# x in a ring of five tiles, loads in pairs, four stores a tile and products in place: a bilinear interaction kernel on one core

## The chip, the cores and the metric

The kernel runs on one core of one Trainium2 chip. The metric is device time in microseconds (us), the median over several executions; lower is better. Each run comes with a state: in the slow one, the cores show a lower clock and the time is some per cent longer.

## The reference

For 4096 samples of 32 features with 64 numbers each, every pair i < j of features (496 pairs) has its own 64 x 64 matrix W. The output is (x_i W_p) * x_j for every pair p, in float32.

```python
idx_i, idx_j = np.triu_indices(F, k=1)          # F = 32: 496 pairs
vi = inputs[:, idx_i, :]
vj = inputs[:, idx_j, :]
vidots = jnp.einsum('bpd,pde->bpe', vi, W)      # W: (496, 64, 64)
return vidots * vj                              # 4096 x 496 x 64 float32, 520 MB
```

42 MB are read and 520 MB are written, so this is a kernel of stores.

## The kernel before

A tile is 128 samples; two tiles are a block. TensorE turns a tile of x, multiplies it with W into PSUM, and VectorE multiplies each PSUM result by x_j into an output buffer. For seven values of i, ScalarE copies the PSUM result to a temporary and GpSimd multiplies it by x_j instead. When a group of pairs is complete, SyncE stores the buffer. There are three output buffers of 105 pairs and five stores a tile.

```python
bounds = [0, p0[3], p0[6] + CH, p0[11], p0[17], NP]     # five groups a tile
xpool = ctx.enter_context(tc.tile_pool(name="xpool", bufs=2))    # two blocks of x
opool = ctx.enter_context(tc.tile_pool(name="opool", bufs=3))
...
        if i in aside and c0 == 0:                      # i = 1, 3, 5, 7, 9, 11, 13
            tmp = dst
            if t >= LEAD:
                tmp = tpool.tile([P, CH, 2, E2], F32, tag="tmp", name=f"tmp_{s}")
            nc.scalar.copy(tmp, src)
            nc.gpsimd.tensor_mul(dst, tmp, xj)
        else:
            nc.vector.tensor_mul(dst, src, xj)
```

Half of the later blocks are loaded by one DMA on ScalarE's queue. The other half are loaded by GpSimd in four DMAs: 120 rows, a tiny read into a scratch tile, and the last 8 rows in two halves. Their names in the code (`load_fifteen`, `turn_engines`) say that this is meant to spare one of the 16 DMA engines; the traces have no engine numbers.

```python
def load_fifteen(blk: int):
    rows = rows_of(x, blk).rearrange("(p k) f d -> p k f d", k=NB)
    dst = xs[blk]

    def part(ps: slice, fs: slice):
        tc.keep_in_program_order(nc.gpsimd.dma_start(out=dst[ps, :, fs, :], in_=rows[ps, :, fs, :]))

    part(slice(0, SWR), slice(0, F))                    # 120 rows
    turn_engines(1)                                     # the scratch read
    for h in range(2):                                  # 8 rows, in two halves of the features
        part(slice(SWR, P), slice(h * F // 2, (h + 1) * F // 2))
```

Two words that come up often: a DMA has "landed" when all its bytes are in place and it raises its semaphore, a counter on which an engine can wait; a queue is "drained" when nothing is left in it.

## Time and profile before

| | before |
|---|---|
| median time | 1333.64 us (4 runs, 1333.56 to 1333.72) |
| busy share: PE, DVE, ACT, POOL | 86%, 72%, 35%, 42% |
| DMA engines | busy from start to end, mean 424 GB/s |
| stores | 161, of 928 to 3360 KB |
| loads of x after the lead | 14 events: 7 on ScalarE's queue, 7 by GpSimd |

PE is TensorE, DVE is VectorE, ACT is ScalarE, POOL is GpSimd. A busy share averages over the span, and here the row that stays full in every slice is that of the DMA engines: the kernel ends when the bytes are out. Any change then has two ways to act: on the rate at which bytes move, and on moments in which nothing is queued for them.

### The profile page before, as it was taken

What the parts mean: (1) busy time and instruction counts of PE and PEld (TensorE: products, weight loads), DVE (VectorE), ACT (ScalarE), POOL (GpSimd) and SP (SyncE); (2) the same over time, 40 slices, a digit from 0 to 9 for tenths busy, and PEclk for the clock granted to TensorE, in tenths of its full rate; (3) what the DMA queues carried; (4) which work ended last, traced back from release to release, by engine and by line L of the source; (5) the groups of instructions that cost most, each with busy time, mean ns of one, the idle gap of its engine ahead of it and who ended that gap; (6) DMA issues with size and microseconds to landing.
All of it is one profiled execution on the core that took longest, in us unless ns stands there. A gap on an engine that the chain in (4) does not pass through costs nothing.

```text
span 1329.5 us, 16690 instructions
## 1 busy us (share of the span) xinstructions
PE 1139.7 (86%) x6656; PEld 605.9 (46%) x6656; DVE 950.9 (72%) x1258; ACT 471.7 (35%) x627; POOL 558.4 (42%) x264
## 2 busy tenths in 40 slices
PE   6989879878898888888989888888897988879994
PEld 4555435444444444444444444444444444444442
DVE  5878768757777677776768777676775777767774
ACT  4463323333333333333333333333333333333331
POOL 1752424444433444333453334533335443444432
PEclk9999999989999899998999999999998999989997
DMA  9999999999999999999999999999999999999998
GB/s 390 432 404 425 428 423 431 426 429 430 420 428 425 431 430 417 430 422 429 431 419 428 424 433 429 416 430 423 431 431 417 430 418 429 431 415 432 429 427 371
DMA packets 28142, 563.13 MB, mean 424 GB/s; under 512 B 3760, under 2 KB 3760, under 8 KB 4112
## 3 DMA queue, kind: packets, MB, share of 16 engines
q1 hardware_dynamic: 24192, 532.69, 94.2%
q0 software_dynamic: 2864, 14.70, 2.7%
q10 hardware_dynamic: 1008, 14.68, 2.6%
q8 instruction: 52, 0.85, 0.2%
q14 instruction: 26, 0.21, 0.0%
HBM read 41.94 MB, written 520.09 MB: 423 GB/s over the span
## 4 chain that ended last, share of the span: by engine, by line
DMA 55%; PE 19%; DVE 15%; POOL 4%; issue 4%; ACT 1%; DVEq 0%; POOLq 0%; SPq 0%; ACTq 0%
DMA out_dram<-ot 55%; PE ps L259 17%; DVE ot L279 15%; POOL ot L277 4%; PE ptx L159 1%; POOL rp L139 1%; ACT tmp L276 0%; DMA xs<-in_r_inputs_dram 0%; PE ptw L148 0%; DVE rp L139 0%; DVEq L279 0%; ACT xT L163 0%; ACT xT L164 0%; ACT xT L165 0%; POOLq L277 0%
## 5 line engine op out<-in xcount | busy, mean ns | idle before, releaser
L279 DVE TENSOR_TENSOR ot<-ps,xs 128x1024 f32<-128x1024 f32 (+15 forms) x1248 | 936.0, 806 | 348.7 <-DMA out_dram<-ot 193.4
L259 PE MATMUL ps<-wT,xT 64*128 64x512 f32 (+12 forms) x6016 | 1049.0, 489 | 157.4 <-DVE ot L279 152.5
L259 PEld LDWEIGHTS ps<-wT,xT 64*128 64x128 f32 x6016 | 535.9, 196 | 609.9 <-DVE ot L279 366.4
L277 POOL TENSOR_TENSOR ot<-tmp,xs 128x1024 f32<-128x1024 f32 x203 | 479.2, 2361 | 693.6 <-ACT tmp L276 520.0
L276 ACT COPY tmp<-ps 128x1024 f32<-128x1024 f32 x203 | 205.5, 1012 | 472.9 <-PE ps L259 436.6
L163 ACT COPY xT<-ptx 128x512 f32<-128x512 f32 x128 | 75.0, 586 | 318.3 <-PE ptx L159 318.3
L159 PE MATMUL ptx<-ident,xs 128*128 128x128 f32 x512 | 84.4, 288 | 9.9 <-DMA xs<-in_r_inputs_dram 6.5
L159 PEld LDWEIGHTS ptx<-ident,xs 128*128 128x128 f32 x512 | 54.0, 141 | 82.2 <-DVE ot L279 57.4
L165 ACT COPY xT<-ptx 64x512 f32<-64x512 f32 x128 | 74.6, 582 | 1.6
L164 ACT COPY xT<-ptx 64x512 f32<-64x512 f32 x128 | 73.9, 577 | 1.5
L277 POOL TENSOR_TENSOR ot<-ot,xs 128x1024 f32<-128x1024 f32 x21 | 49.9, 2378 | 52.2 <-ACT ot L276 52.1
L276 ACT COPY ot<-ps 128x1024 f32<-128x1024 f32 x21 | 21.3, 1013 | 24.4 <-PE ps L259 15.1
L148 PE MATMUL ptw<-ident,rp 128*128 128x128 f32 (+1 forms) x128 | 18.9, 303 | 5.8 <-DVE rp L139 5.8
L148 PEld LDWEIGHTS ptw<-ident,rp 128*128 128x128 f32 (+1 forms) x128 | 16.1, 159 | 14.6 <-DVE rp L139 5.2
L139 DVE COPY rp<-raw 128x1024 f32<-128x1024 f32 x9 | 14.7, 1650 | 10.6 <-DMA raw<-in_L_rec_W_dram 10.6
L151 ACT COPY wT<-ptw 128x1024 f32<-128x1024 f32 (+1 forms) x15 | 14.8, 984 | 13.8 <-PE ptw L148 10.9
L105 POOL DMA_DIRECT2D xs<-in_r_inputs_dram x21 | 13.3, 637 | 0.0
L97 POOL DMA_DIRECT2D scratch<-in_r_inputs_dram x9 | 8.2, 911 | 0.3 <-issue 0.3
L139 POOL COPY rp<-wT 112x1024 f32<-112x1024 f32 x4 | 7.9, 1978 | 0.0
L139 ACT COPY rp<-raw 128x1024 f32<-128x1024 f32 x3 | 6.0, 1987 | 1.9 <-DMA raw<-in_L_rec_W_dram 1.9
L151 DVE COPY wT<-ptw 128x1024 f32<-128x1024 f32 x1 | 1.2, 1225 | 3.0 <-PE ptw L148 3.0
L163 ACT ACT_TABLE_LOAD x1 | 1.3, 1283 | 0.7 <-PEq L303 0.7
(6 smaller groups left out, 0.9 us busy)
## 6 DMA issues: line engine op xcount, KB each, us to landing
out_dram<-ot SPq DMA_DIRECT2D x64, 3360.0 KB, 16.4
out_dram<-ot SPq DMA_DIRECT2D x32, 3168.0 KB, 15.6
out_dram<-ot SPq DMA_DIRECT2D x32, 3104.0 KB, 17.0
out_dram<-ot SPq DMA_DIRECT2D x31, 2880.0 KB, 17.0
xs<-in_r_inputs_dram ACTq DMA_DIRECT2D x7, 2048.0 KB, 18.7
xs<-in_r_inputs_dram POOLq DMA_DIRECT2D x7, 1920.0 KB, 25.0
raw<-in_L_rec_W_dram SPq DMA_DIRECT2D x3, 2048.0 KB, 13.8
xs<-in_r_inputs_dram SPq DMA_DIRECT2D x2, 1024.0 KB, 10.4
```

Source lines behind the costliest of these rows:

```text
L105: tc.keep_in_program_order(nc.gpsimd.dma_start(out=dst[ps, :, fs, :], in_=rows[ps, :, fs, :]))
L139: ins = copy(rp[:r], src[:, k * EU : (k + 1) * EU])
L148: nc.tensor.transpose(pt[:, n, :r], rp[:r, n].rearrange("p h d -> p (h d)"), ident[:r, :r])
L151: copy(home_of(c, r)[:, :, k * EU : (k + 1) * EU], pt[:, :, :r].rearrange("p e r -> p r e"))
L159: nc.tensor.transpose(pt[:, u, :], xs[blk][:, k, f : f + 2, :].rearrange("p f d -> p (f d)"), ident)
L163: copy(xT[:, 0], pt)
L164: copy(xT[D:, 1], pt[:D])
L165: copy(xT[:D, 1], pt[D:])
L259: nc.tensor.matmul(ps[:, h, lo - pa : hi - pa, :], xT[blk, kt, i // RUN][h * D : (h + 1) * D, (i + h) % 2, i % RUN // 2, :], wT[home][h * ...
L276: nc.scalar.copy(tmp, src)
L277: nc.gpsimd.tensor_mul(dst, tmp, xj)
L279: nc.vector.tensor_mul(dst, src, xj)
```

## The change

Its intent: x gets a ring of five tile slots in one long buffer in place of two block buffers, so that two blocks can be loaded together, on two queues, once every four tiles. What that and the in-place products free in memory goes to larger output buffers (127 pairs), and so to four stores a tile. The lead (the first three tiles, in which W is also turned and whose groups are made in turns) gets six groups instead of five. `load_fifteen` keeps its four DMAs but writes into the ring. Cut to its core:

```diff
-    bounds = [0, p0[3], p0[6] + CH, p0[11], p0[17], NP]
+    lead = [0, p0[3], p0[6], p0[9], p0[13], p0[18], NP]
+    later = [0, p0[4], p0[9], p0[15] + 10, NP]
...
-    xpool = ctx.enter_context(tc.tile_pool(name="xpool", bufs=2))
-    tpool = ctx.enter_context(tc.tile_pool(name="tpool", bufs=4))
-    opool = ctx.enter_context(tc.tile_pool(name="opool", bufs=3))
+    xb = const.tile([P, 5 * FD + 3 * GAP], F32, tag="xb", name="xb")
+    ob = const.tile([P, 3 * cap1, D], F32, tag="ob", name="ob")
...
-        dst = xs[blk]                       # in load_fifteen
+        dst = x_block(blk)
...
-    LATE = 6
-    loads = {place[blk * NB, LATE]: blk + 1 for blk in range(2, NBLK - 1)}
+    LATE = 1
+    loads = {place[2 * NB * e - 1, LATE]: 2 * e for e in range(1, NBLK // 2)}
...
         if s in loads:
-            new_x(loads[s])
-            if loads[s] in fifteen:
-                load_fifteen(loads[s])
-            else:
-                load_x(loads[s], nc.scalar)
+            load_x(loads[s], nc.scalar)
+            load_fifteen(loads[s] + 1)
...
-            tmp = dst
-            if t >= LEAD:
-                tmp = tpool.tile([P, CH, 2, E2], F32, tag="tmp", name=f"tmp_{s}")
-            nc.scalar.copy(tmp, src)
-            nc.gpsimd.tensor_mul(dst, tmp, xj)
+            nc.scalar.copy(dst, src)
+            nc.gpsimd.tensor_mul(dst, dst, xj)
```

## The prediction

> **What bounds the kernel now.** I read the slices of the page first, then its DMA queues, then the chain, then stretches of the span side by side.
>
> ```profile
> span 1329.5 us, 16690 instructions
> PE 1139.7 (86%) x6656; PEld 605.9 (46%) x6656; DVE 950.9 (72%) x1258; ACT 471.7 (35%) x627; POOL 558.4 (42%) x264
> ...
> DMA  9999999999999999999999999999999999999998
> ...
> q1 hardware_dynamic: 24192, 532.69, 94.2%
> q0 software_dynamic: 2864, 14.70, 2.7%
> q10 hardware_dynamic: 1008, 14.68, 2.6%
> ...
> DMA 55%; PE 19%; DVE 15%; POOL 4%; issue 4%; ACT 1%; DVEq 0%; POOLq 0%; SPq 0%; ACTq 0%
> ```
>
> The 16 DMA engines are busy from start to end (94.2 + 2.7 + 2.6% for stores, SP's loads and x), and no compute engine is above 86%. So the bytes set the end: 563.13 MB, which the change leaves as they are. What can move is the rate and the idle time of the DMA engines. Five stretches, as busy time of each engine, then granted clock, DMA share and GB/s:
>
> ```profile
> 199.50:262.30 62.80, 56.86 (x348) 30.42 (x350) 48.65 (x70) 22.35 (x31) 25.28 (x11) 0.97 1.00 431
> 262.30:281.20 18.90, 12.97 (x62) 6.24 (x58) 9.09 (x9) 5.79 (x7) 7.07 (x3) 0.91 1.00 419
> 350.80:382.80 32.00, 26.31 (x145) 14.57 (x144) 21.89 (x28) 10.46 (x15) 15.49 (x9) 0.89 1.01 418
> 90.00:95.00 5.00, 5.00 (x38) 2.73 (x36) 3.13 (x6) 3.77 (x5) 3.79 (x2) 1.00 0.62 264
> 1315.00:1329.50 14.50, 0.00 (x0) 0.00 (x0) 0.00 (x0) 0.00 (x0) 0.00 (x0) 0.50 0.68 293
> ```
>
> Stores alone run at 431 GB/s, near 430 over all stretches without loads. A load on ScalarE's queue costs (1 - 419/431) x 18.9 = 0.5 us, one on GpSimd's queue (1 - 418/431) x 32 = 1.0 us: 7 + 7 of them, some 10 us. 563.13 MB at 430 is 1310 us, so all losses together are 20 us: 10 in loads, about 5.5 in the first 125 us (nearly 3 of it the hole around 80 to 95 us), 4 in the uneven end. That is all that a change which moves no bytes can win.
>
> **What the change adds is a wait, and only the order of instructions shows it.** The second of two blocks is loaded by GpSimd in four DMAs: 120 rows, a 4-byte scratch read, then 8 rows in two halves. Before, the halves went out back to back. After, the last of the four waits for the third to land (semaphore names cut):
>
> ```
> before: 8x2x1024 load, 8x2x1024 load, multiply, multiply
> after:  8x2x1024 load (raises SW7 to 16), WAIT SW7 >= 16, 8x2x1024 load, multiply i=1, multiply i=3
>         SyncE: store of the tile's first group waits for GpSimd's count = that second multiply
> ```
>
> The halves do not overlap, but they interleave over the two rows of a partition, so their ranges do; the dependency tracking over one long buffer takes that for a write after a write. It is so in all seven loads. GpSimd's in-place multiplies stand behind it, and a tile's first group cannot be stored without two of them. How long such a wait is, the kernel before shows in the GpSimd timeline (start, duration) and in the DMA issues (KB each, us to landing):
>
> ```profile
> 349.22 0.79 POOL L105 DMA_DIRECT2D xs<-in_r_inputs_dram  x1
> 350.00 0.99 POOL L97 DMA_DIRECT2D scratch<-in_r_inputs_dram  x1
> 350.99 1.14 POOL L105 DMA_DIRECT2D xs<-in_r_inputs_dram  x2
> 352.15 2.37 POOL L277 TENSOR_TENSOR ot<-tmp,xs 128x1024 f32<-128x1024 f32 x1
> ...
> xs<-in_r_inputs_dram POOLq DMA_DIRECT2D x14, 64.0 KB, 28.7
> ```
>
> A half lands 28.7 us after its issue, yet GpSimd multiplies at 352.15, at once. Why so long for 64 KB shows in the queues between 353 and 371 us:
>
> ```profile
> q1 hardware_dynamic: 261, 5.55, 73.5%
> q0 software_dynamic: 260, 1.93, 25.5%
> ```
>
> 261 packets of the store queue, 260 of GpSimd's: they take turns packet by packet, though a store's packet is three times as long.
>
> **What the Trainium skill says.** "DMA: Bandwidth & Descriptors", section "Queues, rings and completion order": each DMA engine goes round-robin between queue rows at packet granularity; the 261 to 260 agree. The same page, section "Anatomy of one DMA — SWDGE (gpsimd) path": DMA engines do not wait on semaphores; the wait happens on the issuing sequencer before dispatch. "PSUM — Partial Sum Buffer", section "Engine vs sequencer instructions": GpSimd's queue is strict FIFO. Together: the multiplies stand still. No trace here shows a GpSimd DMA waiting yet; the one of after will. The first page, section "Issuing engines are not separate DMA queues", says that issuing on two queues saves only issue time, so I expect no bandwidth from "two queues".
>
> **The change, part by part.**
>
> *Four stores a tile.* 161 stores become 18 + 1 + 29 x 4 = 135. From the packets of the trace a store packet takes about 8 ns + 0.0368 ns a byte, its completion 9 ns; a store costs each DMA engine 8 x 8 + 9 = 75 ns beyond its bytes. 26 fewer: -1.9 us.
>
> *Loads in pairs.* Seven events for fourteen. If two loads side by side share the start that costs each 0.5 to 1.0 us: -3 us. Landing is no trouble: issued a whole tile (40 us) ahead.
>
> *Lead of six groups, W turned at other steps.* The hole of nearly 3 us may close, but the buffers of the lead shrink from 105 pairs to 91, which gives less cushion: -1 us, plus or minus 3.
>
> *In-place products.* ScalarE's copy now waits for the output buffer as VectorE's multiply already did. PE is 86% busy, buffers are ahead of the DMA: 0.
>
> *The wait.* Take a load at the start of tile t. One of three output buffers is being filled, so the store queue holds at most two stores. In before, the fifth group's store was issued at 343.45 and the next tile's first group began just after, with about 10 us of stores queued. Scaled to four larger groups (9.6 us each) I estimate 14 us. The loads add 4.2 MB, 9.8 us. So DMA work ends about 24 us after issue. The third DMA stands behind 16 packets of the 120-row load and the scratch read in its ring: at one packet a turn against at most 12 to 14 store packets of 1.19 us, the store queue is always empty before it lands. From then on nothing feeds the DMA engines until the first group is stored:
> - last byte to semaphore, estimated from landings: 1.3 us
> - the last load's issue, half of 1.14: 0.6 us
> - two multiplies of 2.37: 4.7 us, and 0.2 us of semaphores
> - store issue to first packet, 0.8 us (in the hole of the lead it was issued at 91.52, first packet at 92.35)
> - the uneven, short-packet drain of the load queue, a guess: 1.5 us
>
> Sum 9.1 us, six times. In the first load (tile 3) one multiply stands before the wait: 9.1 - 2.4 = 6.7 us. Together 6 x 9.1 + 6.7 = 61 us. Afterwards two groups lie nearly finished and the store of the first (9 us) covers the multiplies of the next (4.7 us), so no second hole follows.
>
> Total: 1333.7 - 1.9 - 3 - 1 + 61 = 1388.8, so 1389 us.
>
> **Rivals.**
> *The wait is hidden* (the third DMA lands while stores are still queued). For it: DMA bound, buffers ahead. Against: three buffers, one of them blocked, give at most 16 store packets an engine, and the wait needs some 20 turns. It would make 1333.7 - 6 = 1328 us.
> *Only the transfer side counts* (pairing collides with stores and slows compute): loads would then slow stores, but the bytes are the same and stores stay queued; 1325 to 1335 us.
> *The wait spreads further* (VectorE and TensorE stall behind GpSimd's multiplies, and a second hole follows each load). VectorE's waits on those counts come in the next uses of a buffer, after the stores; only if the second group were late would this add 3 to 5 us a load: about 1410 us.
>
> **Range and chances.** The wait stands in the built program and each term but two is a measured duration. An error of 2.5 us a load makes 17 us either way: 1372 to 1404. A rival that hides the holes lands within 2%; more than 2% faster would need more than the 20 us of losses there are. Faster 0.01, same 0.08, slower 0.91.
>
> **What would show it.** In the profile after: seven dips in the DMA row, some 160 us apart, each an idle DMA of 7 to 10 us; GpSimd idle 20 us and more before the last of its load DMAs or the multiply after it; DMA share of stretches without loads still 1.00 and near 431 GB/s; 135 stores. If the dips are absent, the ordering argument is wrong; if they are there but of 3 to 5 us, the store queue was deeper or landing quicker than I took it; if they are longer than 12, compute was held up too.

## The result, and the profile after

The changed kernel takes 1394.65 us (4 runs, 1393.76 to 1396.01) against 1333.64 us: 61.0 us more. The ratio is 1.0458, with a 95% interval of 1.044 to 1.0476. Here and below a ratio is the mean time of one kernel's fast runs over that of the other's of the same rounds, so it is not quite the ratio of the medians that are quoted.

The head of the page after, its DMA rows, its queues and its chain:

```profile
span 1392.8 us, 17386 instructions
...
DMA  9999899997999979999799997999979999799998
GB/s 391 431 428 425 293 425 426 434 413 310 437 423 434 414 326 422 435 425 412 314 434 425 433 409 332 423 434 426 416 325 434 426 431 409 333 423 433 425 433 353
...
q1 hardware_dynamic: 20576, 532.69, 90.0%
q0 software_dynamic: 2864, 14.70, 2.9%
...
DMA 50%; PE 20%; issue 11%; DVE 9%; POOL 5%; ACT 3%; DVEq 0%; ACTq 0%; POOLq 0%; SPq 0%
```

The bytes of the store queue are the same 532.69 MB, but that queue now fills 90.0% of the engines' time instead of 94.2%. The DMA row is no longer full. Every fifth slice (35 us each) falls to 293 to 333 GB/s, seven times; the slices between them are as fast as before. That is the shape of seven holes, not of a lower rate. In the chain, "issue" has grown from 4% to 11% and POOL from 4% to 5%.

One hole closely, as stretches with busy time of each engine, then granted clock, DMA share and GB/s:

```profile
325.00:331.00 6.00, 4.58 (x32) 2.56 (x28) 3.26 (x5) 1.02 (x1) 0.00 (x0) 1.00 1.00 418
331.00:340.00 9.00, 5.36 (x24) 3.01 (x26) 3.93 (x6) 2.61 (x3) 5.67 (x4) 0.81 0.06 21
345.00:468.00 123.00, 105.95 (x618) 55.62 (x616) 89.66 (x122) 42.77 (x58) 56.75 (x26) 0.94 1.00 429
```

From 331 to 340 us the DMA engines are 6% busy. What GpSimd does around that time (start, duration, and in brackets how long it sat idle and what the profile thinks ended it):

```profile
294.52 0.80 POOL L152 DMA_DIRECT2D xb<-in_r_inputs_dram  x1
295.31 0.97 POOL L144 DMA_DIRECT2D scratch<-in_r_inputs_dram  x1
296.27 0.56 POOL L152 DMA_DIRECT2D xb<-in_r_inputs_dram  x1
334.31 0.55 POOL L152 DMA_DIRECT2D xb<-in_r_inputs_dram  x1 [37.48 <-DVE ob L313]
334.89 11.60 POOL L311 TENSOR_TENSOR ob<-ob,xb 128x1024 f32<-128x1024 f32 x5
```

GpSimd issues three of the four load DMAs by 296.8 us and then stands still for 37.48 us before the fourth. Then it multiplies five times without a pause, because the work had long been waiting for it. The store of the first group is issued at 339.59 us, when two of these multiplies of 2.36 us are done, and the trace has its first packet at 340.4 us.

The name in the bracket deserves care. The profile puts this wait down to DVE; over all events it names the load itself for most:

```profile
POOL xb L152 <- DMA xb<-in_r_inputs_dram: 201.1, 6, 37.4
POOL xb L152 <- DVE ob L313: 63.8, 2, 37.5
```

A releaser is inferred from what else happened at that moment. The built program says which semaphore that instruction waits on: the one that the third DMA raises when it has landed. (Of the two waits put down to DVE only one is this wait; the other, of 26.4 us, stands before the 120 rows of the first load. The fourth DMA waits 19.5 us at the first load and 34.7 to 37.5 us at the other six.) The experiments decide it.

While GpSimd waits, all three queues drain together. The packets between 300 and 331 us:

```profile
q1 hardware_dynamic: 298, 8.48, 65.7%
q10 hardware_dynamic: 144, 2.10, 16.8%
q0 software_dynamic: 306, 1.98, 16.5%
```

298 packets of stores and 306 of GpSimd's loads: about one each by turns, as before. So a small DMA at the tail of GpSimd's ring lands only when the store queue has given up about as many packets as stand before it.

### The profile page after: what moved, and what is told of

The parts are those of the page before. It is cut to its first block, busy times and chain, and to the rows that moved or that the text cites. A ratio compares the mean times of both kernels' runs of the same rounds, so it can differ in the third digit from the quotient of the medians.

```text
span 1392.8 us, 17386 instructions
## 1 busy us (share of the span) xinstructions
PE 1159.3 (83%) x6644; PEld 611.2 (44%) x6644; DVE 954.0 (68%) x1287; ACT 471.7 (34%) x627; POOL 556.7 (40%) x264
## 3 DMA queue, kind: packets, MB, share of 16 engines
q1 hardware_dynamic: 20576, 532.69, 90.0%
## 4 chain that ended last, share of the span: by engine, by line
DMA 50%; PE 20%; issue 11%; DVE 9%; POOL 5%; ACT 3%; DVEq 0%; ACTq 0%; POOLq 0%; SPq 0%
DMA out_dram<-ob 47%; PE ps L297 18%; DVE ob L313 9%; POOL ob L311 4%; DMA xb<-in_r_inputs_dram 3%; ACT ob L310 2%; PE ptx L200 2%; PE ptw L191 0%; ACT xtb L202 0%; ACT xtb L204 0%; ACT xtb L203 0%; POOL ob L181 0%; DVE ob L181 0%; POOL xb L152 0%; POOL scratch L144 0%
## 5 line engine op out<-in xcount | busy, mean ns | idle before, releaser
L313 DVE TENSOR_TENSOR ob<-ps,xb 128x1024 f32<-128x1024 f32 (+4 forms) x1277 | 941.9, 793 | 404.7 <-DMA out_dram<-ob 217.6
L297 PE MATMUL ps<-wT,xtb 64*128 64x512 f32 (+15 forms) x5760 | 1028.4, 497 | 194.0 <-DVE ob L313 123.9
L297 PEld LDWEIGHTS ps<-wT,xtb 64*128 64x128 f32 x5760 | 520.2, 198 | 667.6 <-DVE ob L313 296.9
L311 POOL TENSOR_TENSOR ob<-ob,xb 128x1024 f32<-128x1024 f32 x224 | 527.2, 2365 | 541.0 <-ACT ob L310 536.8
L310 ACT COPY ob<-ps 128x1024 f32<-128x1024 f32 x224 | 226.9, 1013 | 501.4 <-PE ps L297 302.8
L202 ACT COPY xtb<-ptx 128x512 f32<-128x512 f32 x122 | 71.5, 586 | 353.6 <-PE ptx L200 353.6
L200 PE MATMUL ptx<-ident,xb 128*128 128x128 f32 x512 | 85.8, 291 | 9.2 <-DMA xb<-in_r_inputs_dram 6.4
L200 PEld LDWEIGHTS ptx<-ident,xb 128*128 128x128 f32 x512 | 54.8, 143 | 59.9 <-issue 37.8
L204 ACT COPY xtb<-ptx 64x512 f32<-64x512 f32 x122 | 71.0, 582 | 3.0
L203 ACT COPY xtb<-ptx 64x512 f32<-64x512 f32 x122 | 70.4, 577 | 2.9
L297 PE MATMUL ps<-wT,xb 64*128 64x512 f32 (+15 forms) x244 | 42.4, 465 | 3.4 <-DVE ob L313 1.5
## 6 DMA issues: line engine op xcount, KB each, us to landing
out_dram<-ob SPq DMA_DIRECT2D x3, 2912.0 KB, 12.7
```

Of the source, the lines that this page charges most:

```text
L200: nc.tensor.transpose(pt[:, u, :], x_tile(t)[:, f : f + 2, :].rearrange("p f d -> p (f d)"), ident)
L202: copy(xT[:, 0], pt)
L203: copy(xT[D:, 1], pt[:D])
L204: copy(xT[:D, 1], pt[D:])
L297: nc.tensor.matmul(ps[:, h, :m, :], xT[t, i // RUN][h * D : (h + 1) * D, (i + h) % 2, i % RUN // 2, :], wT[h * D : (h + 1) * D, pa : pa + ...
L310: nc.scalar.copy(dst, src)
```

## The experiments

"Lost in loads" is worked out from the packets of each trace: the length of each load event (from 2 us before its first x packet to 8 us after its last) minus its bytes at 430.1 GB/s, the mean rate of the stretches without loads in the kernel before. "Between" is the same for the stretches between the events, "end" for the last 20 us. The first event holds the end of the lead as well. The start, before the first event, has no column: it loses 5.6 us in before, 4.0 in after, 5.8 in e1 and 4.0 to 6.0 in the others, so single terms of 1 to 2 us differ from run to run.

| kernel | median us (range) | ratio to before, 95% | lost in loads | between | end |
|---|---|---|---|---|---|
| before | 1333.64 (1333.56 to 1333.72) | 1 | 10.4 | 0.1 | 4.3 |
| after | 1394.65 (1393.76 to 1396.01) | 1.0458 (1.044 to 1.0476) | 71.2 | 2.9 | 5.6 |
| e1_rows | 1333.11 (1331.17 to 1334.3) | 0.9991 (0.9978 to 1.0004) | 9.7 | -0.7 | 8.3 |
| e2_moved | 1328.87 (1328.4 to 1329.36) | 0.9962 (0.9947 to 0.9977) | 9.6 | -1.6 | 5.4 |
| e3_before_wait | 1387.08 (1386.24 to 1388.6) | 1.0399 (1.0384 to 1.0413) | 65.3 | 2.4 | 4.7 |
| e4_before_inplace | 1333.81 (1332.4 to 1335.22) | 1.0 (0.9987 to 1.0012) | 11.5 | 2.4 | 4.3 |
| e5_rows_five | 1337.89 (1337.17 to 1339.8) | 1.0031 (1.0018 to 1.0044) | 12.4 | 2.0 | 8.1 |
| e6_rows_split | 1335.51 (1335.13 to 1337.28) | 1.0013 (0.9999 to 1.0027) | 10.1 | 2.5 | 8.4 |
| e7_rows_moved | 1332.27 (1331.19 to 1335.31) | 0.9991 (0.9978 to 1.0003) | 9.8 | -0.5 | 8.0 |
| e8_stagger | 1401.1 (one run) | none | 75.6 | 1.6 | 5.9 |
| e9_no_i1_i3 | 1365.16 (1360.42 to 1370.07) | 1.0235 (1.0213 to 1.0258) | 46.0 | 2.8 | 5.3 |
| e10_no_i3 | 1382.0 (1380.62 to 1382.8) | 1.036 (1.0346 to 1.0374) | 58.1 | 2.9 | 5.6 |
| e11_moved_again | 1330.19 (1328.78 to 1330.93) | 0.9968 (0.9954 to 0.9982) | 10.4 | -1.9 | 6.4 |

The times of before in the three batches were 1333.78, 1333.78 and 1333.56 us. All of e1 to e11 gave correct results. Each batch ran on a chip of its own (e1 to e4, e5 to e8, e9 to e11), with runs of before beside it, so differences of 2 to 5 us between batches are near the noise.

### e1: the wait taken out

```diff
-        for h in range(2):
-            part(slice(SWR, P), slice(h * F // 2, (h + 1) * F // 2))
+        for k in range(NB):
+            tc.keep_in_program_order(
+                nc.gpsimd.dma_start(out=dst[SWR:P, k : k + 1], in_=rows[SWR:P, k : k + 1])
+            )
```

A partition of a block holds two rows of x. Split by feature, each half takes a piece of both rows, and the ranges of the two halves cross. Split by row, they lie one behind the other. The built program then has no wait between them. (In the kernel before, the same crossing halves had no wait either. Why the tool that places the waits adds one when they lie in one long buffer, no run here shows.)

> The changed kernel with the last 8 rows split by row of a partition instead of by half of the features: the two small loads no longer interleave, so the second has no wait on the first; bytes, engines and everything else stay. Theory of the wait: seven idle holes of 6 to 9 us in the DMA row vanish, and 1394.7 us falls by 55 to 61 us, to 1333 to 1340 us (the prediction's own terms without the wait gave 1328). Rival, pairing of loads or in-place products or fewer stores cost the time: stays above 1385 us with the holes in place.

Measured: 1333.11 us, 61.5 us less than after. The loads lost 9.7 us instead of 71.2. GpSimd's timeline at the second load:

```profile
285.67 0.83 POOL L152 DMA_DIRECT2D xb<-in_r_inputs_dram  x1
286.50 1.01 POOL L144 DMA_DIRECT2D scratch<-in_r_inputs_dram  x1
287.51 1.07 POOL L158 DMA_DIRECT2D xb<-in_r_inputs_dram  x2
298.69 2.37 POOL L313 TENSOR_TENSOR ob<-ob,xb 128x1024 f32<-128x1024 f32 x1 [10.12 <-ACT ob L312]
```

Both small loads leave at once, and the next multiply runs at 298.69 us, as soon as ScalarE has made its product. The small loads land later than in before (28.7 us after their issue), by a median of 38.9 us:

```profile
xb<-in_r_inputs_dram POOLq DMA_DIRECT2D x14, 64.0 KB, 38.9
```

A slow landing costs nothing if no engine with work in hand waits for it. The wait explains the slowdown; the rival, that one of the other parts of the change cost the time, falls, because they are all still here.

### e2: the wait kept, but moved behind the multiplies

```diff
         part(slice(0, SWR), slice(0, F))
         turn_engines(1)
-        for h in range(2):
-            part(slice(SWR, P), slice(h * F // 2, (h + 1) * F // 2))
+        part(slice(SWR, P), slice(0, F // 2))
+        return lambda: part(slice(SWR, P), slice(F // 2, F))
...
-            load_fifteen(loads[s] + 1)
+            rest[s + 40] = load_fifteen(loads[s] + 1)
+        if s in rest:
+            rest.pop(s)()
```

> The changed kernel with the interleaved halves and the wait kept, but the last of the four load DMAs issued 40 steps later in the same tile, behind that tile's multiplies on GpSimd. Theory, that it is the multiplies behind the wait and not the wait or the transfer: as fast as without the wait, 1333 to 1340 us, no holes. Rival, the interleaved small transfers themselves or GpSimd's idle time cost: above 1385 us.

Measured: 1328.87 us. The halves still interleave and the fourth DMA still waits for the third in the program, but it comes after the tile's multiplies:

```profile
330.43 2.35 POOL L313 TENSOR_TENSOR ob<-ob,xb 128x1024 f32<-128x1024 f32 x1 [1.28 <-ACT ob L312]
332.72 0.58 POOL L152 DMA_DIRECT2D xb<-in_r_inputs_dram  x1
```

By then the third has landed, and GpSimd does not pause at this load. At the first load it still stands for 9.2 us, yet that event loses 2.6 us against 2.4 in e1, where it does not stand. So it is not the halves that cost, and a pause does not cost by itself: what costs is that multiplies which a store needs stand behind it.

### e3: the wait alone, put into the kernel before

```diff
         for h in range(2):
-            part(slice(SWR, P), slice(h * F // 2, (h + 1) * F // 2))
+            part(slice(SWR, P), slice(max(0, h * F // 2 - 1), (h + 1) * F // 2))
```

> The kernel before with the second small load widened by one feature, so that it truly overwrites a little of the first and must wait for it; nothing else changed. Theory of the wait: about 6 us of idle DMA at each of seven loads (one multiply behind the wait, a store queue of some 11 us at the issue), so 1333.6 + 42 = 1375 us, in 1360 to 1385 us. Rival, the wait only hurts together with paired loads: within 5 us of 1333.6 us.

Measured: 1387.08 us, 53 us more than before, with no other part of the change. The mechanism holds and the rival falls, but my 1375 us was too low, and the result lies just outside the range that I gave. GpSimd and one stretch of the DMA engines:

```profile
350.56 0.58 POOL L105 DMA_DIRECT2D xs<-in_r_inputs_dram  x1
351.16 2.37 POOL L277 TENSOR_TENSOR ot<-tmp,xs 128x1024 f32<-128x1024 f32 x1
369.47 0.59 POOL L105 DMA_DIRECT2D xs<-in_r_inputs_dram  x1 [15.94 <-DMA xs<-in_r_inputs_dram]
370.08 4.66 POOL L277 TENSOR_TENSOR ot<-tmp,xs 128x1024 f32<-128x1024 f32 x2
...
360.00:366.00 6.00, 5.76 (x30) 3.40 (x30) 4.33 (x7) 1.16 (x2) 0.00 (x0) 0.72 1.02 316
366.00:374.00 8.00, 5.73 (x38) 3.05 (x40) 4.89 (x8) 3.62 (x5) 4.51 (x3) 1.00 0.27 85
```

Here the profile names the load as the releaser. In the before kernel a GpSimd load event loses 1.0 us, here 8.2 to 9.1: the wait costs about 7.7 us a load where I had put 6, with 7 of them. The trace accounts for some 1.1 us of the difference: the stores end before GpSimd's load does, and of a load's 240 packets of 8192 B, 38 to 75 then take over 0.5 us each, against 0.31 us beside stores. The DMA share stays full, but the rate falls (1.02 and 316 GB/s from 360 to 366 us). The rest may be the ragged drain of GpSimd's own ring, which I had counted in the prediction and left out here; that is not shown.

### e4: in-place products alone

The `tmp` lines of before are replaced by those of after, for all tiles; nothing else.

> The kernel before with ScalarE's products multiplied in place for all tiles, the third part of the change alone. Theory: no cost, 1333.6 us plus or minus 4. Rival, ScalarE now waits for the output buffer and holds up its x copies: more than 10 us slower.

Measured: 1333.81 us, ratio 1.0 (0.9987 to 1.0012). This part is free here, as predicted; what it is worth is the memory of the temporaries.

### e5 and e6: four stores or five, loads together or apart, both without the wait

```diff
# e5, on top of e1
-    later = [0, p0[4], p0[9], p0[15] + 10, NP]
+    later = [0, p0[3], p0[6] + CH, p0[11], p0[17], NP]
-    cap1 = max(b - a for a, b in groups[LEAD])
+    cap1 = 127
# e6, on top of e1
             load_x(loads[s], nc.scalar)
-            load_fifteen(loads[s] + 1)
+        if s in loads2:                       # one tile later
+            load_fifteen(loads2[s])
```

> e1 (no wait, rows) with five stores a tile at the old cuts instead of four. Theory, each store costs each DMA engine 75 ns beyond its bytes: 29 stores more, 2.2 us slower than e1, about 1335 us, and 430 instead of 431 GB/s between loads. Rival, larger stores gain nothing or the smaller buffers cost cushion: equal to e1 within 1 us, or slower by over 4 us.

> e1 with the second block of a pair loaded one tile later, so the loads are not side by side. Theory, loads in pairs share part of what each costs (in the trace 1.1 to 1.2 us a pair against 1.5 us for two single loads): 2 to 3 us slower than e1, about 1336 us. Rival, pairing gains nothing: equal to e1 within 1 us.

Measured: e5 takes 1337.89 us, 4.8 us more than e1. In the profiled runs 2.7 us more than in e1 are lost between the loads, near the 2.2 us that 29 stores of 75 ns make, and another 2.7 us in the load events (the start loses 1.7 us less). So smaller groups also seem to bridge the loads less well. The 4.8 us are over the threshold that I had set for the rival of a smaller cushion: both seem to be at work, though e1 is of another batch. e6 takes 1335.51 us, 2.4 us more than e1, as I had expected, but not where I had expected it: its load events lose only 0.4 us more than e1's, and 3.2 us lie between them, over 1 us of it in two short stretches between the loads of a pair (813.0 to 822.7 and 974.6 to 987.0 us, DMA share 0.95 and 0.93). The intervals of e1 and e6 overlap a little, so that pairing saves 2.4 us is likely but not firm; that it does so because two loads share their start is not shown.

### e7: why e2 was faster than e1

e1 with its last small load issued 40 steps later, as in e2.

> e1 (rows, no wait) with the last small load moved 40 steps later, as in e2. It tells why e2 (1328.9) was faster than e1 (1333.1), whose slowest DMA engine ends 8 us behind the middle one, e2's 4 us. Theory A, the time of the small load: about 1329 us. Theory B, the shape of the small loads (one row of 8 KB against two halves of 4 KB a DMA engine): about 1333 us.

Measured: 1332.27 us (1331.19 to 1335.31), which is e1's time and not e2's. So the difference (3.4 us to e2, 2.1 us to e2's repetition e11, both of other batches) does not come from when the small load is sent but, it seems, from its shape: all kernels with rows (e1, e5, e6, e7) lose 8.0 to 8.4 us in the last 20 us, those with halves 4.3 to 6.4. By the last 16 completions of the store queue, one DMA engine of e1 ends some 8 us behind the middle one. Which engine it is, and why one row of 8 KB instead of two halves of 4 KB should load it more, the trace does not show, for it has no engine numbers. It stays open.

### e8: is the rate lower because the engines run in step?

Between the holes of after, the DMA engines make 428 to 431 GB/s (in five stretches 429, 428, 429, 430, 431) where e1 makes 430 to 431; over some 930 us that would be 2 to 3 us. After a hole all engines start the same store at nearly the same moment (first packets at 340.42 to 340.57 us), so I tried to bring them out of step with four tiny extra loads on few of the engines.

```diff
+        if s - 30 in stagger:                 # half a tile after each hole
+            o = starts[4] if stagger[s - 30] % 2 else starts[0]
+            for lo, hi in ((0, 8), (8, 16), (16, 20), (20, 22)):
+                nc.scalar.dma_start(out=xb[lo:hi, o : o + FD], in_=x[lo:hi].rearrange("p f d -> p (f d)"))
```

> The changed kernel as it is (holes in place) with four tiny extra loads into a free tile, half a tile after each hole, that hold up some DMA engines by 0.3 to 1.2 us and others not. Theory, after a hole all 16 DMA engines run in step and the stores then go at 428 instead of 431 GB/s, which is some 5 us of the 61 us lost: the stretches behind the extra loads go at 430 to 431 GB/s; the time stays within 5 us of 1394.7 us, for the held-up engines end later. Rival, the lower rate has another cause: 428 GB/s as before.

Measured: 1401.1 us in a single run of unknown state, 6.4 us above after where I had allowed 5 (the extra loads move 1.26 MB, 2.9 us), and 429 to 430 GB/s in the five stretches behind the extra loads, as in after. The theory that they run in step is not supported; the small term between the holes is unexplained.

### e9 and e10: how the hole adds up

The wait is left as it is, and GpSimd is given fewer products in the first group of a tile (VectorE makes them instead).

```diff
-    aside = (1, 3, 5, 7, 9, 11, 13)
+    aside = (5, 7, 9, 11, 13)          # e9
+    aside = (1, 5, 7, 9, 11, 13)       # e10
```

> The changed kernel with its wait in place, but the two products of a tile's first group (i = 1 and 3) made by VectorE, so that the first group's store no longer stands behind GpSimd. Theory: GpSimd waits as long as before, but the first group's store, 9 us of DMA work, is queued in time and covers most of the landing and of the two multiplies of the second group: holes of 0 to 3 us instead of 9, 1334 to 1355 us. Rival, GpSimd standing still or the small loads cost by themselves: above 1385 us.

> The changed kernel with only i = 3 made by VectorE: one multiply of 2.4 us behind the wait instead of two before the first group's store. Theory, the hole is a sum in which each multiply counts in full: six holes shorter by 2.4 us (14 us) and the first, where no multiply is left behind the wait, shorter by 5 to 9 us: 1371 to 1376 us, in 1366 to 1380. Rival, the hole is one fixed delay of the load: 1390 us and more. Rival, VectorE's added work costs: no fall either.

e10 measured 1382.0 us, 12.7 us less than after, and so outside of my 1366 to 1380. The six later events fell from 59.5 to 47.1 us in sum, 2.1 us each, which is nearly the full multiply of 2.36 us: it counts as the sum says. The first event, where I had expected 5 to 9 us, fell by 0.7 us only; the trace shows why:

```profile
170.91 0.58 POOL L152 DMA_DIRECT2D xb<-in_r_inputs_dram  x1 [25.65 <-DMA xb<-in_r_inputs_dram]
171.51 9.28 POOL L311 TENSOR_TENSOR ob<-ob,xb 128x1024 f32<-128x1024 f32 x4
```

Without i = 3 the first group's store goes out in time, at 147.77 us. But the second group needs the products of i = 5 and 7, which stand behind the fourth load, so its store is issued only at 176.21 us, two multiplies after the wait. The hole has moved from one group to the next. The same happens in e9, whose first event fell by 0.5 us.

e9 measured 1365.16 us: 29.5 us less than after, though GpSimd waits longer than ever:

```profile
338.93 0.56 POOL L152 DMA_DIRECT2D xb<-in_r_inputs_dram  x1 [40.41 <-DMA xb<-in_r_inputs_dram]
...
325.00:339.00 14.00, 9.13 (x48) 4.75 (x44) 5.59 (x8) 3.04 (x3) 0.07 (x1) 0.74 1.03 434
339.00:346.00 7.00, 7.00 (x48) 3.64 (x46) 5.76 (x9) 2.95 (x5) 6.98 (x4) 1.00 0.43 182
```

The first group's store keeps the DMA engines at 434 GB/s up to 339 us, past the point where the hole of after begins. Then the second group's store has to wait for the fourth load and two multiplies, and a shorter hole follows. GpSimd stands longer and the kernel loses less, so the rival (GpSimd standing still costs by itself) falls. But I had expected holes of 0 to 3 us and 1334 to 1355 us; six events lost 5.0 to 6.4 us each, some 4.6 us over e1's 1.2. I take it that the added store also takes turns with the small load and so moves its landing back: GpSimd stood 40.41 us instead of 37.48.

### e11: the version that beats both

e2 once more, in five rounds on another chip.

> e2 once more in five rounds, as the version that beat both kernels: 1328.9 us again, 0.3 to 0.5% faster than before with an interval clear of 1. If it was a chance of that chip's runs: 1332 us and more, as e1 and e7.

Measured: 1330.19 us (1328.78 to 1330.93), ratio 0.9968 (0.9954 to 0.9982). It is 0.3% faster than before, and in both runs (e2 and e11) the interval leaves out 1. This is the changed kernel with one DMA issued later: what is left of its gain once the wait is out of the way.

## Why the prediction was right

The predicted 1389 us (1372 to 1404, slower with 0.91) stands against 1394.65 us, and e1, e2 and e3 show that its reason was the right one. By its steps:

- **The bound.** Right. Between the holes the DMA share is 1.00 at 429 GB/s. 61 us of added loss became 61 us of added run time.
- **The wait.** Predicted 61 us, measured 61.5 (after against e1, both as times and as the loss in load events). Its terms in the hole at 331 to 340 us: from the end of the drain (about 331.5) to the fourth load's issue at 334.31 it took 2.8 us, against 1.3 + 1.5 predicted; the issue 0.6; two multiplies 4.7; store issue to first packet 0.8. Sum 8.9 us against 9.1. Over the six later events the loss over e1's is (59.5 - 7.2) / 6 = 8.7 us. That the whole fits to 0.5 us is in part luck: each of the six came out 0.4 us shorter than the sum of 9.1 us, and the first load 2.6 us longer than its 6.7.
- **The first load.** Wrong in size: predicted 6.7 us because one multiply stands ahead of the wait, measured 11.7 - 2.4 = 9.3 us. The multiply did run ahead (at 142.69 us), and the hole itself is some 6 us long. The prediction had the path before it wrong, for it let the loads move at the full rate to their end. Here no store is issued between 139.26 and 167.50 us, the store packets are over by 154 us, and the rest of GpSimd's load runs alone:

```profile
155.00:162.00 7.00, 3.95 (x28) 2.21 (x26) 3.69 (x6) 2.38 (x3) 0.00 (x0) 1.00 0.91 190
162.00:168.00 6.00, 5.43 (x36) 2.54 (x32) 2.69 (x6) 2.88 (x5) 3.48 (x3) 1.00 0.07 16
```

  Its packets of 8192 B take 0.61 us (median) from 155 to 162 us and 0.31 us beside stores. At 190 instead of 430 GB/s the 7 us lose 3.9 us, though the DMA share is 0.91.
- **When the load is issued.** Wrong, with little effect. I let it start with the tile and gave it 24 us of queued work. GpSimd has nothing to do in a tile's last group, and the slots that it overwrites are free by then, so it issues a group earlier (294.5 us, while the last group's store is issued at 304.0). It therefore stands still for 37.48 us, but the hole is the same, since the landing follows the drain in either case.
- **Stores.** Predicted -1.9 us. Without the wait the stretches between loads are 0.8 (e1) to 1.7 us (e2) shorter, and e5 puts 2.7 us on 29 stores. Right within what can be read; the 8 ns a packet are not firm, for a fit to the medians of before's packets gives 8.9 ns and one to after's 0.6 ns. In the changed kernel itself the term does not show: its stretches lose 2.9 us.
- **Pairs of loads.** Predicted -3 us. The load events of e1 lose 9.7 us against 10.4. The six later pairs cost 1.2 us each, against 0.4 to 0.6 plus 1.0 to 1.1 us for two single loads of before, so some 0.3 us a pair are saved; but the first event, where the lead runs dry, loses 2.4 us against 1.0 for the first two loads of before. e6 gives pairing 2.4 us, but mostly elsewhere.
- **Lead.** Predicted -1 plus or minus 3. The start of after loses 4.0 us instead of 5.6, and the old hole at 90 us is gone, but at the lead's end, 135 to 140 us, the DMA share is 0.83, and in e1, with the same lead, the start loses 5.8 us. No gain in sum.
- **What was left out: the end.** The last 20 us lose 5.6 us instead of 4.3, and 8.3 with the rows of e1.
- **Slips in the sums,** none of which changes the result: 8 x 8 + 9 is 73 and not 75 ns; 2.5 us at seven loads is 17 us, so the upper end should be 1406 us and not 1404; the scratch read moves 0.1 KB by the trace and not 4 bytes.

The gains that I had summed to -5.9 us came to -0.5 us in e1 and to -4.8 and -3.4 us in the two runs of the moved version. That is in the main why the result lies 5.7 us above the prediction although the wait was sized within 1 us.

The rivals: "the wait is hidden" fell on the seven dips; "only the transfer side counts" fell on e1; "the wait spreads further" asked for a second hole or longer ones, and the stretch from 345 us on is full.

## What to carry to other kernels

A DMA that waits on a semaphore held up GpSimd here, with everything behind it, for up to 37.5 us; so after moving a buffer into another allocation, compare the waits of the built program on each engine that issues DMAs, not only the diff. A kernel bound by its stores can afford such a wait as long as the queued stores outlast it (9.2 us at the first load of e2, without loss), and it pays for every step between the last byte and the next store once the queue runs dry: here landing, one issue, two multiplies and a store. A full DMA share is not yet a full rate: 190 GB/s at a share of 0.91 when a load ran alone. When two transfers must go to one region, cut it so that their address ranges do not cross, or send the second after the work that cannot wait.

## What the Trainium skill lacked or had wrong

- "DMA: Bandwidth & Descriptors", section "Queues, rings and completion order", has the turns by packet right (298 store packets to 306 load packets, 261 to 260 before). It does not draw the consequence, to which the runs fit: how late a small DMA lands is set by the packets before it in its own ring times the packet length of the other queues. 64 KB landed after 28.7 us in before, beside one queue of long store packets, and after 38.9 us in e1, beside stores and a second load.
- The same page, section "SWDGE vs HWDGE vs iDMA", calls a packet of GpSimd's DMAs "≤4096 B preferably" and gives no size for those of SyncE. In these traces a packet of GpSimd's 120-row load has 8192 B, each row of a store counts as one packet of up to 32,512 B, and the turns go by those.
- The same page, section "Anatomy of one DMA — SWDGE (gpsimd) path", says that waits happen on the issuing sequencer, and "PSUM — Partial Sum Buffer", section "Engine vs sequencer instructions", that GpSimd is strict FIFO. Neither says what follows for arithmetic on that engine: 19.5 us without a multiply at the first load, 34.7 to 37.5 us at each of the others, 61.5 us in the whole kernel.
- The first of these pages gives a DMA a fixed cost of about 2 us, as latency, and a floor of about 10.5 ns a packet for small loads. It doesn't give what one more store costs when the queue is full: by an estimate from the packets some 75 ns on each DMA engine (8 ns for each of 8 rows and 9 ns for the completion); in e5 29 stores cost 2.7 us between loads.
- No page says that a load's packets slow down when they run alone: those of 8192 B on GpSimd's queue took 0.31 us beside stores and 0.61 us without, and the rate fell to 190 GB/s at a DMA share of 0.91.
- "DMA: Bandwidth & Descriptors", section "Where 436 GB/s comes from", says that for transfers between HBM and SBUF the HBM side (~358 GB/s) binds. With one core at work, stores ran at 428 to 432 GB/s in the stretches without loads or holes; the page "HBM Reference", section "Specifications (TRN2)", has it right, that a core alone goes well above its share.
